# Weights of the values prepared one unit earlier through the projections' buffers, and the first loads of the values moved beside the first attention

## The chip, the core and the metric

The kernel is one program on one core of a Trainium2 chip. The metric is device time in microseconds (us). Before the change three runs gave 2971.14 us as the median, with 2968.95 and 2975.28 us at the ends. The profiled execution, from which all durations here come, took 2968.51 us.

## What is computed

The reference chains four blocks on an activation `x` of 8 sequences of 112 tokens with 512 channels, all in float32, and a context of 8 sequences of 375 tokens with 512 channels:

```
x = L0(x, ctx)        # cross attention, one head:  x + alpha * softmax(q k^T / sqrt(C)) v Wo
x = L1(x, ctx)        # layer norm, token mixing, a scan over time with a 16 x 16 state per head, channel mixing
x = L2(x, ctx)        # the same with other weights
x = L3(x, ctx, ctx)   # layer norm + cross attention (16 heads of 128, keys and values from ctx) twice, then an MLP
```

The change concerns L0, and the part of L3 that needs only the context: the values `ctx @ wv1`, `ctx @ wv2` (512 to 2048 columns each) and a group of the keys. They don't depend on `x`, so the kernel computes them as filler work while L1 and L2 run.

## The kernel before, in words

**The values (`values`, L818).** The generator covers five sets of weights: four pairs of groups of 512 columns of `wv1` and `wv2`, and one pair of `wk1`. A set has 12 units (the last has 3), one for each pair of sequences and third of their tokens, 51 in all. A unit multiplies 2 x 2 blocks with seven products in place of eight; the products are called k1, k6, k7, k2, k8, k5, k9. Each needs one operand of 256 x 512 from the weights (four raw blocks a11, a21, a22, a12, of which one is overwritten, and sums of them: a21 + a22, s1, s2, s3) and one block of the context. The context's blocks and their sums were written to memory during L0 by `park` (L249), and come back as `cv` tiles through `load` (L882). A product is two matmuls of 128x128 by 128x512 (L906). ACT copies its PSUM bank to SBUF (L931, L999, L1013), POOL adds copies (L932), and SP stores the results (L922 to L926). There are two PSUM banks, used in turn; k1, k6, k7 and k8 add up in one bank, with a copy out between them.

**The filler.** L1 and L2 call `fill(n)` at many points, and each call emits n pieces of the generator (one piece is one product with its copies). Inside `time_mix` (L549) a manual schedule makes all engines but SP follow the written order; elsewhere a planner decides each engine's order when the program is built. All engines execute their own queue in order. Every DMA is issued on SP's queue; they take eight semaphores in turn, so a transfer is issued only after the one eight before it has landed.

**A new set of weights.** Seven buffers `w` hold a set's operands. The first set is loaded by `weights(0)` (L841): four loads of 512 KB (L839), then four sums on POOL (L846 to L849). `weights(2)` does the same between L1 and L2. The other three changes of set happen in the middle of `time_mix` and are done by `relay` (L852): from the last-but-one unit of the old set on, three raw blocks lie in two buffers of the projections' pool `wpool` (four buffers of 128 x 2048), POOL writes a sum or a copy into a buffer of the old set as soon as that one's last product has been issued (L862, L864, L868, L874, and the copy L876), and three raw blocks are loaded a second time into freed buffers of `w`. `after` (L965) counts the products and triggers each step.

**The scan (`time_mix`).** There are 64 steps per layer: 4 groups of channels (`c`) with 16 steps (`at`). Per step, ACT copies `vp` to PSUM (L588, L589), DVE multiplies (L687) and scans (L691, `st`, two buffers), POOL multiplies `rs` (L695, six buffers), and every four steps PE sums four `rs` (L668, `ps_y`), always two steps behind. Each step also has one or two pieces of filler. From `at` = 2 of the next group on, the group norm of the finished one runs beside it (L607 to L634).

**L0 (`layer0`, L225).** Its pools, in order of their SBUF addresses: `keep` (identity, transposed weights, w_qk, q, z, w_vo), `work` (the context's tiles `cx`, four buffers, and small tiles), and in PSUM first the two `mm` banks, then the attention's six. After eight attentions the output projection `ps_o` (L161) runs in the two `mm` banks and DVE adds it to `x` (L350). When L0's pools close, the values' pool and its two banks take the lowest addresses.

## Time and profile before

| what | before |
|---|---|
| three runs: median (ends) | 2971.14 us (2968.95, 2975.28) |
| the profiled execution | 2968.51 us |
| its span | 2966.1 us (2.4 us lie around it) |
| PE (matmul) busy | 2861.6 us, 96% |
| DVE busy | 1610.9 us, 54% |
| ACT busy | 998.9 us, 34% |
| POOL busy | 876.4 us, 30% |
| mean DMA rate | 136 GB/s |
| granted TensorE clock, mean | 0.988 |
| L0's attentions and projection | 62 to 157 us |
| L1's 64 steps of the scan | 366 to 623 us |
| L2's 64 steps of the scan | 986 to 1247 us |

The profile gives, for each engine, when it was busy, how long it sat idle before an instruction and which engine or transfer ended that idle time. Matmul records are half-matmuls in this program: one matmul of 128x512 in float32 shows as two records, and a product of the values as four. A line of a timeline is: start, length, engine, source line, operation, output<-inputs, shape, count, and in brackets the idle time before it with its releaser.

### The profile page before, as it was taken

The page shows a single profiled execution, that of the slowest core. Times are in us where ns is not written, and L with a number is a line of the kernel's source. Part 1 is how long each engine was busy: PE and PEld are TensorE (multiplying, and loading weights), DVE is VectorE, ACT ScalarE, POOL GpSimd, SP SyncE. Part 2 cuts the span into 40 slices and gives each one's busy share as a digit, 9 for nine tenths or more (in the row PEclk, how much of TensorE's full clock was granted, in tenths as well). Part 3 has the DMA queues.
Part 4 walks back from the last instruction along what each step waited for, and adds up shares of the span by engine and source line. Part 5 has one row for each costly group of instructions (what it writes and reads, how often), then busy time and mean ns, then how long its engine had stood idle before and what let it go on. Part 6 is the DMA issues. An engine that isn't in the chain of part 4 may idle for free.

```text
span 2966.1 us, 29798 instructions
## 1 busy us (share of the span) xinstructions
PE 2861.6 (96%) x10130; PEld 1561.7 (53%) x10130; DVE 1610.9 (54%) x2350; ACT 998.9 (34%) x1992; POOL 876.4 (30%) x702
## 2 busy tenths in 40 slices
PE   8979999999999999999899999999999999999999
PEld 4734443344444433356465666666565656656544
DVE  1563288857342688743455554545554554545455
ACT  2123355533233555532332323232331323323311
POOL 2142078754231588732411010100302010000030
PEclk9989999999999999999999999999999999999999
DMA  6421398944321889742344344334233433432110
GB/s 255 150 89 45 116 291 247 282 135 126 96 68 54 246 251 271 225 141 70 130 130 128 129 128 129 108 119 140 88 120 102 144 108 119 140 114 77 42 54 25
DMA packets 199318, 402.90 MB, mean 136 GB/s; under 512 B 33288, under 2 KB 119592, under 8 KB 192384
## 3 DMA queue, kind: packets, MB, share of 16 engines
q1 hardware_dynamic: 199168, 401.01, 43.0%
q8 instruction: 81, 1.33, 0.2%
q14 instruction: 69, 0.57, 0.1%
HBM read 323.16 MB, written 77.91 MB: 135 GB/s over the span
## 4 chain that ended last, share of the span: by engine, by line
PE 80%; DVE 7%; POOL 4%; issue 3%; ACT 3%; DMA 2%; SPq 0%; DVEq 0%; POOLq 0%; ACTq 0%
PE ps_vk L906 13%; PE ps_k1k L1134 10%; PE ps_k5k L1134 7%; PE av L1303 6%; PE sc L1290 5%; PE ps_o L161 3%; PE pt L1293 3%; PE ps_fk L161 2%; PE ps_k1q L1061 2%; PE ps_k L484 2%; PE ps_r L484 2%; PE ps_k5q L1061 2%; PE ps_k7q L1061 2%; PE ps_fr L161 2%; PE ps_k5o L1061 1%
## 5 line engine op out<-in xcount | busy, mean ns | idle before, releaser
L906 PE MATMUL ps_vk<-wv,cv 128*128 128x512 f32 x1328 | 597.0, 600 | 29.5 <-DMA wv<-in_L_xattn_wv 8.2
L906 PEld LDWEIGHTS ps_vk<-wv,cv 128*128 128x128 f32 x1328 | 249.3, 191 | 361.7 <-issue 301.8
L932 POOL TENSOR_TENSOR k<-k,k 128x512 f32<-128x512 f32 (+1 forms) x153 | 201.7, 1318 | 306.7 <-ACT k L931 261.6
L691 DVE TENSOR_TENSOR_SCAN st<-decay,kv 128x904 f32<-128x904 f32 x128 | 260.7, 2037 | 16.7 <-POOL rs L695 4.0
L695 POOL TENSOR_TENSOR rs<-st,r 128x896 f32<-128x896 f32 x128 | 246.7, 1928 | 55.3 <-DVE st L691 42.4
L218 ACT ACTIVATE prob<-sc,top 112x376 f32<-112x376 f32 (+1 forms) x264 | 151.8, 575 | 322.6 <-DVE top L215 195.2
L1303 PEld LDWEIGHTS av<-pts,v 125*128 125x128 f32 (+1 forms) x1536 | 185.7, 193 | 31.0 <-DVE pts L1299 16.0
L1290 PE MATMUL sc<-k,q 128*112 128x376 f32 x512 | 201.1, 485 | 0.7 <-ACT prob L218 0.7
L1283 POOL COPY k<-over_k 128x4 f32<-128x4 f32 x64 | 13.8, 224 | 604.7 <-PE sc L1290 576.7
L1303 PE MATMUL av<-pts,v 125*128 125x112 f32 (+1 forms) x1536 | 190.0, 278 | 1.8 <-DVE pts L1299 0.9
L1134 PE MATMUL ps_k1k<-cs,wsk 128*128 128x375 f32 x480 | 178.6, 481 | 1.5 <-ACT p1k L1137 1.5
L215 DVE TENSOR_REDUCE top<-sc 112x1 f32<-112x376 f32 (+1 forms) x264 | 143.5, 545 | 64.3 <-PE sc L1290 51.9
L687 DVE TENSOR_TENSOR kv<-vp,k 128x904 f32<-128x904 f32 x128 | 141.5, 1105 | 64.8 <-ACT vp L589 59.0
L931 ACT COPY k<-ps_vk 128x512 f32<-128x512 f32 (+1 forms) x153 | 89.2, 583 | 183.1 <-PE ps_vk L906 180.2
L999 ACT COPY k<-ps_vk 128x512 f32<-128x512 f32 (+1 forms) x153 | 89.1, 582 | 153.6 <-PE ps_vk L906 148.7
L1293 PEld LDWEIGHTS pt<-ident_l,prob 112*125 112x125 f32 (+1 forms) x768 | 97.8, 176 | 72.0 <-DVE prob L220 43.9
L1293 PE MATMUL pt<-ident_l,prob 112*125 112x112 f32 (+1 forms) x768 | 121.4, 277 | 2.5 <-DVE prob L220 1.9
L220 DVE TENSOR_SCALAR prob<-prob,total 112x376 f32<-112x376 f32 (+1 forms) x264 | 118.3, 448 | 8.0
L1134 PEld LDWEIGHTS ps_k1k<-cs,wsk 128*128 128x128 f32 x480 | 89.5, 190 | 59.4 <-ACT p1k L1137 1.8
L589 ACT COPY vp<-vj 128x896 f32<-128x896 f32 x124 | 112.8, 910 | 7.0 <-DMA vj<-rows 3.1
L1141 DVE TENSOR_TENSOR k<-ps_k5k,u2k 128x375 f32<-128x375 f32 x52 | 28.5, 548 | 159.2 <-PE ps_k5k L1134 158.2
L1310 DVE TENSOR_TENSOR ctxt<-av,bv 128x448 f32<-128x448 f32 x64 | 39.9, 624 | 128.8 <-PE av L1303 128.8
(384 smaller groups left out, 4800.6 us busy)
## 6 DMA issues: line engine op xcount, KB each, us to landing
vj<-rows SPq DMA_DIRECT2D x124, 448.0 KB
cv<-blocks SPq DMA_DIRECT2D x181, 251.5 KB
cs<-blocks SPq DMA_DIRECT2D x120, 375.0 KB
wvs<-k SPq DMA_DIRECT2D x128, 256.0 KB
v<-wvs SPq DMA_DIRECT2D x64, 512.0 KB
cx<-in_ctxT SPq DMA_DIRECT2D x38, 750.0 KB
v<-wvs SPq DMA_DIRECT2D x64, 252.0 KB
wvs<-k SPq DMA_DIRECT2D x64, 224.0 KB
```

Of the source, the lines that this page charges most:

```text
L161: nc.tensor.matmul(p, w[:, k, o * P : (o + 1) * P], rhs(k, h), start=k == 0, stop=k == NC - 1)
L215: nc.vector.tensor_reduce(top, scores, AX.X, ALU.max, negate=True)
L218: nc.scalar.activation(prob, scores, AF.Exp, bias=top, accum_out=total)
L691: nc.vector.tensor_tensor_scan(flat(st), flat(decay[:, c]), flat(kv), 0.0, ALU.mult, ALU.add)
L695: nc.gpsimd.tensor_mul(by_batch(rs), st[:, :, :L], by_batch(r[:, c, :]))
L906: nc.tensor.matmul(to, left, right, start=start and n == 0, stop=k == 1, skip_group_check=True)
L932: nc.gpsimd.tensor_add(y, z, y)
L1061: nc.tensor.matmul(to, lhsT, rhs, start=start and k == 0, stop=k == 1, skip_group_check=not start)
L1134: nc.tensor.matmul(y, lhsT, rhs, start=start and k == 0, stop=k == 1, skip_group_check=True)
L1290: nc.tensor.matmul(sc, q[:, o, tok], kt[:, o, :], start=True, stop=True)
L1293: nc.tensor.transpose(pt[t][:nt, o, :], prob[:, t0 : t0 + nt], ident[:L, :L])
L1303: nc.tensor.matmul(av[:, o, :], v[:nt, t, o * HD : (o + 1) * HD], pts[:nt, t, o, :], start=t == 0, stop=t == 2,)
```

## The change

It does two things, and swaps two allocations.

1. In L0, the context's tiles get a pool of their own (`near`), which now has the lowest SBUF addresses; `z` and `w_vo` get a pool (`last`) behind `keep`; and in PSUM the attention's banks come before the `mm` banks. So the buffers and banks that the values' pool takes over are ones that the attention uses, not ones that the output projection uses.
2. For the changes of set that happen inside L1's and L2's scans with `at` = 0 and 2, `relay` is replaced by the new `ahead`, which starts one unit sooner (unit 9 of 12). It takes three buffers of `wpool`, loads the four raw blocks once, makes three sums there and one in the old k1's buffer, and then ACT copies six operands of 128 x 1024 from `wpool` into the old set's buffers, one after each of the following products. The next set's first products (k1, k6, k7, k2 of its first unit) read the operands in `wpool`. The change of set at `at` = 3 still uses `relay`.
3. In `time_mix`, `early` is allocated ahead of `w_o`.

```diff
         with (
+            tc.tile_pool(name="a0s", bufs=2, space=PSUM) as ps2,
+            tc.tile_pool(name="a0c", bufs=4) as near,
             tc.tile_pool(name="a0", bufs=1) as keep,
+            tc.tile_pool(name="a0z", bufs=1) as last,
             tc.tile_pool(name="a0w", bufs=2) as work,
             tc.tile_pool(name="a0p", bufs=2, space=PSUM) as ps,
-            tc.tile_pool(name="a0s", bufs=2, space=PSUM) as ps2,
...
-                cxs[b] = work.tile([P, NC, S], F32, tag="cx", name=f"cx0_{b}", bufs=4)
+                cxs[b] = near.tile([P, NC, S], F32, tag="cx", name=f"cx0_{b}")
...
-            z = keep.tile([P, NC, N], F32, name="z0")
+            z = last.tile([P, NC, N], F32, name="z0")
...
-            w_vo = product(turned(w_v, "v"), w_o, "w_vo")
+            w_vo = product(turned(w_v, "v"), w_o, "w_vo", last)
...
+        def ahead(at, old, new):
+            x1, x2, x3 = (wpool.tile([P, NC, C], F32, tag="w", name=f"wx{j}_{at}") for j in range(3))
+            a11, a21, a22, a12, s2, s1 = (x[:, k : k + 2] for x in (x1, x2, x3) for k in (0, 2))
+            for y, o, k in ((a11, 0, 0), (a21, 1, 0), (a22, 1, 1), (a12, 0, 1)):
+                raw(y, at, o, k)
+            new.update(k1=a11, k6=s1, k7=s2, k2=a12, k8=a22, k5=a21, k9=old["k1"])
+            yield "k7", 2
+            nc.gpsimd.tensor_sub(s2, a11, a21)
+            yield "k6", 0
+            nc.gpsimd.tensor_add(a21, a21, a22)
+            yield "k8", 0
+            nc.gpsimd.tensor_sub(s1, a21, a11)
+            yield "k1", 2
+            nc.gpsimd.tensor_sub(old["k1"], a12, s1)
+            free = [("k6", "k1"), ("k7", "k6"), ("k2", "k7"), ("k8", "k2"), ("k5", "k8"), ("k9", "k5")]
+            for last, _ in free:
+                yield last, 1
+                nc.scalar.copy(old[last], new[dict(free)[last]])
+            yield "k1", 0
+            new.update({what: old[last] for last, what in free})
...
-            if unit == UNITS - 2 and at != 1:
+            if unit == UNITS - 3 and at in (0, 2):
+                new = {}
+                steps = ahead(at + 1, s, new)
+                following = next(steps)
+                made.clear()
+            elif unit == UNITS - 2 and at == 3:
                 new = {}
                 steps = relay(at + 1, s, new)
                 ready = next(steps)
-            elif unit == UNITS - 1 and at != 1:
+            elif unit == UNITS - 1 and at == 3:
                 following = ready
                 made.clear()
```

More of the change, by code (lines that the diff above doesn't have):

```diff
@@ L291, in turned, with product @@
                 return t
-            def product(a, b, name, scale=1.0):
-                y = keep.tile([P, NC, C], F32, tag=name, name=name)
+            def product(a, b, name, pool, scale=1.0):
+                y = pool.tile([P, NC, C], F32, tag=name, name=name)
                 for c in range(NC):
@@ L303, in product @@
                 return y
-            w_qk = product(turned(w_q, "q"), turned(w_k, "k"), "w_qk", 1.0 / math.sqrt(C))
+            w_qk = product(turned(w_q, "q"), turned(w_k, "k"), "w_qk", keep, 1.0 / math.sqrt(C))
             q = keep.tile([P, NC, N], F32, name="q0")
-            z = keep.tile([P, NC, N], F32, name="z0")
+            z = last.tile([P, NC, N], F32, name="z0")
             project(
@@ L642, in beside @@
                 return {2: take(c - 1), 3: group_norm(c - 1, g)}
+            early = wpool.tile([P, NC, C], F32, tag="w", name=f"early{n}").rearrange("p k c -> p (k c)")
             w_o = wpool.tile([P, NC, C], F32, tag="w", name=f"w_{pre}Wo")
@@ L648, in time_mix @@
                 )
-            early = wpool.tile([P, NC, C], F32, tag="w", name=f"early{n}").rearrange("p k c -> p (k c)")
             for at in range(3):
```

## The prediction

> **What bounds the kernel now.** I read the page first, then who waited for whom on PE, and then the order of time around each long wait.

> ```profile
> PE 2861.6 (96%) x10130; PEld 1561.7 (53%) x10130; DVE 1610.9 (54%) x2350; ACT 998.9 (34%) x1992; POOL 876.4 (30%) x702
> PE 80%; DVE 7%; POOL 4%; issue 3%; ACT 3%; DMA 2%; SPq 0%; DVEq 0%; POOLq 0%; ACTq 0%
> ```

> PE is the bound nearly everywhere; some 104 us of the span are left to win. The change adds no matmul, so it can only shorten PE's pauses or add to them. In PE's table of waits these belong to the code it touches:

> ```profile
> PE ps_vk L906 <- DMA wv<-in_L_xattn_wv: 8.2, 1, 8.2
> PE ps_vk L906 <- POOL wv L868: 4.8, 2, 2.7
> PE ps_vk L906 <- POOL wv L848: 2.3, 1, 2.3
> PE ps_vk L906 <- POOL wv L876: 1.6, 1, 1.6
> ```

> PE's timeline behind L0's output projection:

> ```profile
> 157.31 0.92 PE L182 MATMUL mean_ln<-part_mean_ln,mean_c 128*128 128x448 f32 x2
> 166.38 2.05 PE L906 MATMUL ps_vk<-wv,cv 128*128 128x512 f32 x2 [8.15 <-DMA wv<-in_L_xattn_wv]
> 168.22 1.70 PE L182 MATMUL var_ln<-part_var_ln,mean_c 128*128 128x448 f32 x2
> 169.71 3.49 PE L906 MATMUL ps_vk<-wv,cv 128*128 128x512 f32 x6
> 175.52 7.30 PE L906 MATMUL ps_vk<-wv,cv 128*128 128x512 f32 x16 [2.32 <-POOL wv L848]
> 186.35 5.91 PE L447 MATMUL ps_t<-xx,maa 128*128 128x448 f32 x8 [3.53 <-DVE xx L438]
> ```

> The filler's first product stands in PE's queue ahead of `var_ln`, so its late weights hold up L1's layer norm too: 14 us of idle in all, at a granted clock of 0.79 (windows, 159 to 186.35).

> **Part 1, the first loads.** SP issued the four `cv` and four `wv` loads from 157.54 on, when `ps_o` had ended, and the first sum began at 167.66: 10.1 us later. In the order of the changed program the first `cv` load waits for the last transposition of the attention (about 130.5), with SP's queue empty since 110. So the operands land near 141, the four sums run until about 151, and at 157.3 PE has work. The constants behind them on SP (4 rows for the biases, 6 for the heads) come earlier; the 14 loads of `maa` and `d`, now behind all these, end near 158 (0.6 us each from 149) and are needed at 177.

> Then the chain, by the rows of before. `mean_ln` now waits for the last addition to `x` (157.51 + 0.68): 158.3 to 159.2. DVE's subtraction 2.0, ACT's squares 1.7, DVE's sum 1.9: 165.1. PE meanwhile runs four products (0.43 us a record, a copy of 0.58 between those that share a bank), so `var_ln` comes at about 165.5. Table load and root 1.9 on ACT, behind two copies: 168.2. Reciprocal 2.94, multiplication 2.0: 173.5. ACT's scaling stands behind the copy of k6 of the second unit and starts at 174.1; before, it started at 183.01. That is 8.9 us, and everything to the mixing follows it (POOL `sx`, DVE `xx`, `ps_t` at 177.5). PE has seven matmuls fewer left beside the mixing, but DVE sets the pace there (22 us of work in 195 to 218), so that costs nothing; if DVE were faster, it would cost 7 x 0.86 = 6.0.

> What it costs: the sums now lie beside `ps_o`. DVE before:

> ```profile
> 170.61 5.34 DVE L180 TENSOR_TENSOR part_mean_ln<-part_mean_ln,x 128x448 f32<-128x448 f32 x2
> 182.91 0.27 DVE L809 TENSOR_TENSOR less_mean_h<-ident_rs,mean_h 128x128 f32<-128x128 f32 x1
> ```

> Two additions that take 0.62 each elsewhere (L178) took 2.67 each while POOL made the same sums. [...] In the new order two additions of the layer norm and two `over` lie between additions to `x` from 143 to 151, and `less_mean_h`, which waits for four small loads, behind them. PE has two banks and 3 us a group, so 2.3 us of lateness is free. If one addition is blocked the projection loses nothing; if each of three is, `x` of the fourth group comes at 151.8 in place of 146.2 and PE loses about 3.4. I take 2.0. The DMA wait's whole 14 us can't be had, since DVE and ACT are late next. Part 1: 8.9 - 2.0 and about 0.6 for DVE pauses in the mixing: **-7.5** (bounds -5 and -10.5).

> **Part 2, the changes of set.** What they cost now is best read from the starts of `ps_y`, one batch for each four steps:

> ```profile
> 1037.10 1.71 PE L668 MATMUL ps_y<-rs,pick 128*32 128x448 f32 x16
> 1052.67 1.71 PE L668 MATMUL ps_y<-rs,pick 128*32 128x448 f32 x16
> ...
> 1101.53 1.71 PE L668 MATMUL ps_y<-rs,pick 128*32 128x448 f32 x16
> 1104.65 1.98 PE L906 MATMUL ps_vk<-wv,cv 128*128 128x512 f32 x4 [1.41 <-ACT k L1013]
> 1108.80 10.55 PE L906 MATMUL ps_vk<-wv,cv 128*128 128x512 f32 x20 [2.16 <-POOL wv L868]
> 1119.18 1.88 PE L906 MATMUL ps_vk<-wx,cv 128*128 128x512 f32 x4
> 1122.67 1.98 PE L906 MATMUL ps_vk<-wv,cv 128*128 128x512 f32 x4 [1.61 <-POOL wv L876]
> 1124.58 1.71 PE L668 MATMUL ps_y<-rs,pick 128*32 128x448 f32 x16
> ```

> In L2 the batch with the change takes 23.05, the same place in another group 15.57: 7.5 us lost. In L1 (497.55 to 519.97, against 433.17 to 452.65) it is 22.42 against 19.48: 2.9 lost. So 10.4 us is the most that can be had.

> Per change POOL loses the copy (1.04) and keeps four sums of 2.35; they move about 20 us earlier, one for each two steps, between the `rs`. There POOL is 77% busy (93 of 120 us in 370 to 490), so two steps of 7.7 leave 1.8: each sum is 0.6 too much, and idle between `rs` is not all usable.

> L1: following POOL's new order from 470.6, `rs` of step 15 ends at 499.9 instead of 494.9. DVE's scan waits for it (two `st` buffers), and PE's batch of 497.55, which has two steps of slack, waits 2.3. It then runs at 503.1 what started at 503.85: a gain of 0.7, and ACT's blocked group norm takes some. I take **-0.5** (bounds +2 and -2.9).

> L2: the same reckoning puts the multiplication that releases ACT (3.88 us idle at 1103.37) 1.5 later, so the wait of 1.41 at 1104.65 becomes 2.9; but the waits for L868, the hidden 1.7 in the row of 10.55, and L876 go. Six ACT copies come in. The trace has the same form at L416, 128x1024 in 1.05 us. A step has two evictions (1.16) and `vp` (1.1): 3.3 with one copy, 4.4 with two, against PE's 3.9. Behind a copy stand the next eviction and `vp`, for which PE and DVE wait; at the one step with two copies and the norm, PE resumes at 1109.0, no sooner than before, and only the later 3.3 us are won. I take **-3.0** (bounds 0 and -7.5). All twelve copies on PE's path would be +12.6; none, 0.

> The raw loads come earlier into buffers that have been free since 380, and three loads of 512 KB per change fall away; SP's later `fWk` and `Wfk` loads have over 100 us. In `weights(2)` a11 is now the block whose buffer comes free last: the four sums end perhaps 8 us later than 727.7, under the channel mixing, which runs on PE until 786. Swapping `early` and `w_o` costs nothing either: PE has filler at the start of the scan. If those covers were gone it would be those 8 us.

> Sum: -7.5 - 0.5 - 3.0 = **-11**. The profiled execution (2968.5) lies 2.6 under the median; I set it on the median: 2971.1 - 11 = **2960.1**.

> **Rivals.** *Everything goes* (0.15): no blocking in L0 (-10) and POOL's and ACT's gaps hold all moved work (-10.4): 2951. For it: POOL's mean share is 30%. Against it: it was saturated from 490 to 518.
> *Only the loads pay* (0.17): `less_mean_h` and the blocked additions cost the full 3.4, so -5.5, and the scan gives back 2: 2967.6. For it: ACT's and POOL's queues each held PE up by 1.4 to 2.7 us at these places. Against it: the longest waits go whole.
> *Slower* (0.05): POOL becomes the scan's bound. Its idle of 0.2 to 1.4 us ahead of each `rs` waits for DVE and can't be filled, so all eight sums (18.8) lie on the loop of scan and `rs`, with half of each copy (6.3) behind them: 25.1 - 10.4 - 7.5 = +7, 2978. It decides from about seven and a half sums on the loop.
> That the loads don't move is excluded by the order of the program.

> **Numbers.** The forecast holds 0.63, its own range 2953 to 2965. Within 0.2% (5.9 us, about what a measurement can tell here) means 2965.2 to 2977.1: mostly the second rival. Faster 0.78, same 0.17, slower 0.05. The range 2951.5 to 2969 leaves out the tail of the first rival and the slower cases.

> **What would show it.** Right: no wait of `ps_vk` for `wv` near 160; the first sum near 141; `ps_t` near 178 to 180; `ps_o` ending 1 to 3 us late with stretched additions on DVE; no L868 or L876 waits before 1300; the L2 batch at 18 to 21 us, the L1 batch near 22 with a wait of `ps_y` for `rs`. Wrong: ACT copies far off 1.05; `vp` waits of DVE at every step with a copy; `ps_t` after 183.

## The result, and the profile after

Eight runs of the changed kernel have a median of 2957.48 us (2954.9 to 2966.74), eight of the kernel before, on the same chip, 2969.68 us (2966.97 to 2975.28). The ratio is 0.9966 with a 95% interval of 0.9955 to 0.9976: 10.1 us faster (7 to 13); the two medians lie 12.2 us apart, inside this interval. The forecast was 11 us. The profiled execution took 2960.41 us, its span 2958.3 us, 7.8 us shorter than before. Why a single pair of profiles shows less than the runs is said under "Right and wrong".

The page's busy times and the engines' shares of the chain that ended last:

```profile
PE 2862.2 (97%) x10130; PEld 1561.7 (53%) x10130; DVE 1603.7 (54%) x2350; ACT 1009.1 (34%) x2004; POOL 872.6 (29%) x700
PE 80%; DVE 7%; POOL 4%; DMA 3%; issue 3%; ACT 3%; SPq 0%; DVEq 0%; POOLq 0%; ACTq 0%
```

PE's work is the same; ACT has twelve instructions and 10 us more (the copies). In PE's table of waits the four lines shown of before are gone. ACT's three lines (`ps_vk` for `k`) have grown from 12.5 us to 14.1 in sum. Of the lines that are new or grew, these two belong to the changed code as well:

```profile
PE ps_o L161 <- DVE x L353: 3.6, 1, 3.6
...
PE ps_y L671 <- POOL rs L698: 3.3, 3, 1.6
```

PE's timeline behind L0's output projection (lines are three higher than before):

```profile
133.47 14.46 PE L161 MATMUL ps_o<-z,w_vo 128*128 128x448 f32 x38
151.56 10.98 PE L161 MATMUL ps_o<-z,w_vo 128*128 128x448 f32 x24 [3.63 <-DVE x L353]
...
163.32 1.02 PE L182 MATMUL mean_ln<-part_mean_ln,mean_c 128*128 128x448 f32 x2
...
182.32 1.02 PE L450 MATMUL ps_t<-xx,maa 128*128 128x448 f32 x2 [1.28 <-DVE xx L441]
```

The waits of 8.15 and 2.32 us, shown in the prediction, have gone, and `ps_t` comes 19.0 us behind `mean_ln`, where it came 29.0 us behind it. But `mean_ln` itself comes 6 us later. The projection waits for DVE, and DVE's timeline shows why:

```profile
142.68 2.73 DVE L180 TENSOR_TENSOR part_mean_ln<-part_mean_ln,x 128x448 f32<-128x448 f32 x1
145.33 5.58 DVE L979 TENSOR_TENSOR over<-over,bv 4x512 f32<-4x512 f32 x2
150.84 0.67 DVE L353 SCALAR_TENSOR_TENSOR x<-ps_o,alpha,x 128x448 f32<-128x448 f32 x1
```

POOL's timeline of the same stretch, with the second and the last of its four sums (139.92 to 150.37):

```profile
142.58 2.35 POOL L850 TENSOR_TENSOR wv<-wv,wv 128x1024 f32<-128x1024 f32 x1
...
147.70 2.67 POOL L852 TENSOR_TENSOR wv<-wv,wv 128x1024 f32<-128x1024 f32 x1
```

Three DVE instructions with two SBUF inputs (one addition, two subtractions `over`) end only about half a microsecond after one of POOL's sums ends. The `x` behind them, for which PE needs the bank, comes 5.9 us late; 2.3 of that are free, as the forecast said, and PE waits 3.6. In L2 the batch with the change of set:

```profile
1091.65 2.12 PE L671 MATMUL ps_y<-rs,pick 128*32 128x448 f32 x16
1095.67 1.98 PE L933 MATMUL ps_vk<-wv,cv 128*128 128x512 f32 x4 [1.91 <-ACT k L1045]
...
1110.36 1.71 PE L671 MATMUL ps_y<-rs,pick 128*32 128x448 f32 x16
```

It takes 18.71 us in place of 23.05; the waits for POOL are gone, those for ACT have stayed.

### The profile page after: what moved, and what is told of

Its sections match the earlier page's. It is cut to its first block, busy times and chain, and to the rows that moved or that the text cites. A ratio compares the mean times of both kernels' runs of the same rounds, so it can differ in the third digit from the quotient of the medians.

```text
span 2958.3 us, 29826 instructions
## 1 busy us (share of the span) xinstructions
PE 2862.2 (97%) x10130; PEld 1561.7 (53%) x10130; DVE 1603.7 (54%) x2350; ACT 1009.1 (34%) x2004; POOL 872.6 (29%) x700
## 4 chain that ended last, share of the span: by engine, by line
PE 80%; DVE 7%; POOL 4%; DMA 3%; issue 3%; ACT 3%; SPq 0%; DVEq 0%; POOLq 0%; ACTq 0%
PE ps_vk L933 13%; PE ps_k1k L1166 10%; PE ps_k5k L1166 7%; PE av L1335 6%; PE sc L1322 5%; PE pt L1325 3%; PE ps_o L161 3%; PE ps_fk L161 2%; PE ps_k1q L1093 2%; PE ps_r L487 2%; PE ps_k L487 2%; PE ps_k7q L1093 2%; PE ps_fr L161 2%; PE ps_k5q L1093 2%; PE ps_k5o L1093 1%
## 5 line engine op out<-in xcount | busy, mean ns | idle before, releaser
L933 PE MATMUL ps_vk<-wv,cv 128*128 128x512 f32 x1296 | 583.7, 601 | 13.9 <-ACT k L1031 6.3
L218 ACT ACTIVATE prob<-sc,top 112x376 f32<-112x376 f32 (+1 forms) x264 | 151.8, 575 | 322.3 <-DVE top L215 194.8
L1031 ACT COPY k<-ps_vk 128x512 f32<-128x512 f32 (+1 forms) x153 | 89.1, 582 | 163.2 <-PE ps_vk L933 156.0
L1173 DVE TENSOR_TENSOR k<-ps_k5k,u2k 128x375 f32<-128x375 f32 x52 | 28.5, 548 | 159.2 <-PE ps_k5k L1166 158.2
```

What stands on the lines that cost most here:

```text
L218: nc.scalar.activation(prob, scores, AF.Exp, bias=top, accum_out=total)
L933: nc.tensor.matmul(to, left, right, start=start and n == 0, stop=k == 1, skip_group_check=True)
```

## The experiments

Eleven kernels were run, each beside runs of the kernel before on its own chip. Microseconds from a ratio are (1 - ratio) x 2970; the intervals are 3 to 5 us wide to either side. So the causes are read from stages of the traces, between landmarks that all kernels have: the first record of `ps_o` (it lies among the last attention's products, 3.6 us ahead of the long row of `ps_o`), the first `mean_ln`, the first `ps_t`, L1's first `ps_y`; and in each scan the stretch from the fourth to the thirteenth `ps_y`, which holds the change of set.

| kernel | ratio to before (95%) | `ps_o` to `mean_ln` | to `ps_t` | to `ps_y` | L1 stretch | L2 stretch |
|---|---|---|---|---|---|---|
| before | 1 | 26.91 | 29.04 | 202.26 | 151.53 | 156.18 |
| changed | 0.9966 (0.9955, 0.9976) | 33.44 | 19.00 | 199.22 | 152.32 | 152.99 |
| p1_loads_only | 0.9975 (0.9961, 0.9988) | 31.01 | 19.01 | 197.56 | 151.56 | 155.84 |
| p2_sets_only | 0.9985 (0.9973, 0.9997) | 26.91 | 29.16 | 202.39 | 151.41 | 152.79 |
| l2_only | 0.9956 (0.9940, 0.9971) | 34.63 | 19.00 | 201.27 | 153.19 | 152.05 |
| l1_only | 0.9981 (0.9967, 0.9995) | 31.75 | 19.00 | 197.52 | 151.25 | 155.83 |
| over_pool | 0.9957 (0.9942, 0.9973) | 35.30 | 19.06 | 200.83 | 152.57 | 152.45 |
| over_first | 0.9953 (0.9936, 0.9970) | 31.95 | 19.01 | 197.71 | 151.25 | 154.98 |
| sums_dve | 0.9945 (0.9928, 0.9962) | 27.96 | 18.99 | 201.14 | 151.51 | 154.94 |
| dve_l2 | 0.9953 (0.9936, 0.9971) | 28.84 | 18.99 | 199.59 | 151.20 | 152.63 |
| dve_loads | 0.9957 (0.9941, 0.9974) | 27.96 | 18.98 | 201.01 | 152.76 | 155.85 |
| copies_dma | 1.0023 (1.0013, 1.0033) | 29.84 | 19.00 | 199.15 | 160.78 | 162.43 |
| copies_twice | 0.9978 (0.9968, 0.9989) | 33.44 | 19.00 | 201.31 | 153.45 | 154.58 |

### Each part alone: p1_loads_only, p2_sets_only

```diff
 # p1_loads_only: the new pools of layer0, and
+            if unit == UNITS - 2 and at != 1:
+                new = {}
+                steps = relay(at + 1, s, new)
 # p2_sets_only: layer0 as before, ahead() for at in (0, 2), early ahead of w_o
```

> The first loads moved beside the first attention, all three changes of set inside the scans as in the kernel before. Theory (each part keeps its own gain): the first ps_y of L1 comes 7.1 us sooner than in the kernel before, as in the changed kernel; the L1 change keeps its batch of 22.4 us and the L2 change its batch of 23.1 us, so the whole is 7 us faster (5 to 9). Rival (the loads' gain is lost again where a later wait takes its place, and the changed kernel's gain comes from the changes of set): 0 to 3 us faster.

Measured: 7.4 us faster (4 to 12). The scans are those of the kernel before, as in the theory. L1's first `ps_y` comes 10.6 us sooner, counted from `ps_o`, 3.5 more than the theory had; 2.9 of these come between the second `var_ln` and the second `ps_t`, where this trace has no slower clock (see "Right and wrong").

> The new changes of set in L1 and L2 and the swap of early and w_o; L0 as in the kernel before, with its wait of 8.1 us for wv. Theory: L1's change gives nothing or loses 0.8 us, L2's gives 3.2 us, so 2 to 3 us faster, and the first ps_y of L1 within 0.5 us of the kernel before. Rival (the loss in L1 in the changed kernel comes from the shifted phase of the loads, not from the new change of set): L1's change gains 0.5 to 3 us here and the whole is 4 to 6 us faster.

Measured: 4.5 us faster (1 to 8). L1's stretch is 151.41 against 151.53, L2's 152.79 against 156.18, as the theory had them; the rival's gain in L1 did not come. The two parts alone add up to 11.9 us, the whole gave 10.1: they add up within what is measured.

### The change of set in one layer alone: l2_only, l1_only

```diff
-            if unit == UNITS - 3 and at in (0, 2):
+            if unit == UNITS - 3 and at in (2,):   # l1_only: (0,)
...
-            elif unit == UNITS - 2 and at == 3:
+            elif unit == UNITS - 2 and at in (0, 3):   # l1_only: (2, 3)
```

> The changed kernel with the old change of set in L1 and the new one in L2 alone. Theory (the new change costs 0.8 us in L1): 0.5 to 1 us faster than the changed kernel, about 11 us faster than the kernel before. Rival (the batches around L1's change are longer because of the earlier start, not because of the copies): slower than the changed kernel by 0.5 to 2.9 us, the batch of L1's change back at 22.4 us.

Measured: 13.1 us faster than before (9 to 18), 3 us more than the changed kernel, with overlapping intervals. The theory had 11. L1's stretch, with the old change of set, was the longest so far, 153.19, which seems to speak against the theory. But PE's clock was halved behind its wait for POOL there (PE's window: from, to, length, busy time, records, granted clock, DMA share, GB/s):

```profile
499.60:503.00 3.40, 3.28 (x4) 0.50 0.86 250
```

That costs 1.7 us, and the batch took 24.08 where the kernel before took 22.42. The trace decides nothing about L1.

> The changed kernel with the new change of set in L1 alone; L2 has the old one. Theory: the stretch of L1 takes 151 to 152.6 us and that of L2 156.0, so it is as fast as the loads alone within 1 us: 7 us faster than before, 2.6 slower than the changed kernel. Rival (L1's change costs 3 us): 3 to 5 us faster than before.

Measured: 5.6 us faster (1.5 to 10). The stretches came as the theory had them (151.25 and 155.83); the time lies between the two. So over all traces: L1's stretch is 152.05 as the mean of the five with the old change (151.20 to 153.19), 151.72 of the six with the new one and single ACT copies (151.25 to 152.57): -0.3, smaller than its own scatter. The scatter of the old change is the clock: 151.20 to 151.56 in the three traces without half clock in this stretch, 152.76 and 153.19 in the two (dve_loads, l2_only) that have 3.4 us of it. So where the clock stays up, the new change gains nothing in L1; it only takes away the wait of 2.7 us for POOL, behind which the clock fell in two of five traces. L2's is 155.93 in four (155.83 to 156.18) and 153.26 in seven (152.05 to 154.98): -2.7, outside its scatter.

### What held up the projection: over_pool, over_first, sums_dve

```diff
 # over_pool
-            nc.vector.tensor_sub(over, over, bv)
+            nc.gpsimd.tensor_sub(over, over, bv)
 # over_first: loads and subtraction of over stand ahead of load(m) and weights(0), the stores stay behind
 # sums_dve
-            nc.gpsimd.tensor_sub(s2, a11, a21)
...
+            eng = nc.gpsimd if at else nc.vector
+            eng.tensor_sub(s2, a11, a21)
...
```

> The changed kernel with the two small subtractions of the values' biases (over, 4x512) on POOL behind its four sums, where DVE made them between the additions to x of L0's projection. Theory (DVE's two-input instructions stand blocked behind POOL's sums and hold up the last addition to x, for which PE waited 3.6 us): that wait goes, ps_o ends near 157 in place of 162.4, ps_t of the mixing starts 3 to 5 us sooner, and the whole is 3 to 5 us faster than the changed kernel. Rival (POOL's reads slow down DVE's additions to x themselves, or the clock of PE sets the end): ps_o ends after 160.5 and the time is within 1.5 us of the changed kernel.

Measured: `mean_ln` came 35.30 us behind the first `ps_o`, later than in the changed kernel (33.44) and in all six traces with its L0 (29.84 to 34.63); the time is 12.8 us under before, not to be told from the changed kernel's. The stall had not gone, it had moved. SP's timeline and ACT's:

```profile
153.04 0.26 SPq L981 DMA_DIRECT2D overs<-over  x1
...
157.61 0.31 ACT L811 ACTIVATE mean_h<-same 128x128 f32<-128x128 f32 x1 [22.53 <-DMA same<-in_heads]
```

The stores of `over` now wait on SP for POOL (until 153.0), and three of the four loads `same` of the heads stand behind them in SP's queue; ACT's `mean_h` waits for these, DVE's `less_mean_h` for ACT, and the next `x` behind it in DVE's queue for that. The run says nothing for or against the theory; it shows the chain of queues.

> The changed kernel with the loads and the two subtractions of the biases (over) ahead of the loads of the first set; the stores of over stay behind. So they run before POOL's sums, and the loads of the heads no longer stand behind a store that waits for over. POOL's sums come about 2 us later, near 142 to 152. Theory (three blocked instructions in a row held up the additions to x): only additions of the layer norm and the copies of pick stand beside the sums, at most one between two additions to x; PE's wait for DVE x is under 1.5 us and ps_t 3 to 5 us sooner than in the changed kernel. Rival (any instruction that reads SBUF is stretched, pick too, and two of them lie between two additions to x): the wait stays at 2 to 4 us and nothing is gained.

Measured: 14.0 us faster than before (9 to 19). PE's wait is 2.14 us and `mean_ln` comes at 31.95, only 1.5 us sooner than in the changed kernel and inside the range of the six traces with its L0. With `over` out of the way, other instructions of DVE stretched in its place, and not only ones with two inputs:

```profile
147.96 2.37 DVE L807 COPY ones_t<-heads 128x128 f32<-128x128 f32 x1
150.25 2.62 DVE L816 COPY pick<-heads 128x32 f32<-128x32 f32 x4
```

In the changed kernel, behind POOL's last sum, they take 0.20 and 0.46. The rival is right in this: these copies from SBUF to SBUF were stretched too.

> The changed kernel with the four sums of the first set of weights made by DVE in place of POOL. A DVE sum of 128x1024 is taken at 1.16 us (the multiplication of 128x1792 takes 2.02), and between two additions to x of the projection DVE has 2.3 us free. Theory (what the changed kernel lost on ps_o is POOL's reads blocking DVE's two-input instructions, and the slower clock after PE's pause): no wait of ps_o for DVE above 1 us, ps_o 27 to 28 us from its first record to mean_ln (33.4 in the changed kernel, 26.9 before), no addition above 0.8 us, ps_t 5 to 6 us sooner and the whole 5 us (3 to 6) faster than the changed kernel. Rival (the sums wait for the late operands at about 141 and hold DVE's queue, whichever engine makes them): ps_o still 30 us or more, and the time within 2 us of the changed kernel.

Measured: 16.3 us faster than before (11 to 21). PE's timeline, and DVE's:

```profile
134.25 23.59 PE L161 MATMUL ps_o<-z,w_vo 128*128 128x448 f32 x62
```

```profile
141.95 1.22 DVE L851 TENSOR_TENSOR wv<-wv,wv 128x1024 f32<-128x1024 f32 x1
143.08 0.62 DVE L178 TENSOR_TENSOR part_mean_ln<-x 128x448 f32<-128x448 f32 x1
```

The projection runs through without a wait, a DVE sum takes 1.22 us (POOL 2.35 to 2.67), no addition is stretched (the one of `part_mean_ln` takes 0.62, each `over` 0.67), and `mean_ln` comes 27.96 us behind the first `ps_o`: 1.05 more than before, which is the filler's product that stands ahead of it. The theory holds: the stall was POOL's sums against DVE.

### What the copies on ACT cost: copies_dma, copies_twice

```diff
-                nc.scalar.copy(old[last], new[dict(free)[last]])
+                nc.sync.dma_start(old[last], new[dict(free)[last]])      # copies_dma
+                nc.scalar.copy(old[last], new[dict(free)[last]])         # copies_twice: this line twice
```

> The changed kernel with the six copies per change of set made by DMA from SBUF to SBUF in place of ACT, in L1 and L2. If ACT's copies are what is left of the cost of the new change of set (1.05 us each, in ACT's queue ahead of evictions and vp), the four batches of ps_y around L1's change take 1 to 3 us less (152.3 us from the fourth ps_y to the thirteenth in the changed kernel) and so do those of L2 (153.0), and the whole is 2 to 5 us faster. Rival (SP's queue and the DMA engines, 90% busy in the scans, pay for it): vj and cv come late, the scan waits for DMA, and it is 1 to 6 us slower.

Measured: 6.8 us slower than before (4 to 10), some 17 slower than the changed kernel. PE's waits in L1's scan, then in L2's:

```profile
PE ps_vk L933 <- DMA wv<-wx: 4.1, 1, 4.1
```

```profile
PE ps_vk L933 <- DMA wv<-wx: 7.6, 1, 7.6
```

Both stretches grew by 9 us, the waits and the half clock behind them (6.8 us of it in L1's stretch, 10.2 in L2's). The rival was right in kind and too small: the copies by DMA come late for the product that needs them. This run can't show what ACT's copies cost, since they were replaced by something dearer.

> The changed kernel with each of the six ACT copies per change of set issued twice, 12.6 us more of ACT in all. If the copies lie on the path (all of each), it is 12 us slower; if they lie half in ACT's gaps, 4 to 8 us; if ACT has room enough, within 2 us. The forecast's reckoning (3.3 us of ACT for a step with one copy, 4.4 with two, against PE's 3.9) says: about half a microsecond for each doubled copy, 6 us slower, equally in L1 and L2.

Measured: 6.5 us faster than before (3 to 10), 3.6 slower than the changed kernel. The stretches grew by 1.7 us in L1 (153.45 against a mean of 151.72) and 1.3 in L2 (154.58 against 153.26), 3.0 for twelve more copies of 1.05 us: 0.25 us each. It is one trace, and L2's mean has a scatter of 3 us; against the two L2 traces that, like this one, have no half clock there (152.99, 152.05), it is 2.1, which makes 0.3 each. So a quarter to a third of an added copy reaches PE, where the forecast's reckoning had half; the rest lies in ACT's gaps. What the first copy costs need not be the same.

### Combinations: dve_l2, dve_loads

```diff
 # dve_l2 = sums_dve with ahead for at == 2 alone; dve_loads = sums_dve with relay in all three places
```

> The changed kernel with the first set's sums on DVE, and the new change of set in L2 alone (L1 has the old one). Theory (in L1 the new change gains and loses nothing: from the fourth to the thirteenth ps_y 151.8 us with it and 152.1 without, as means over the traces so far): within 1.5 us of the kernel with DVE sums and both changes, 15 to 17 us faster than the kernel before. Rival (in L1 it costs 3 us, as the measured times of the changed kernel and of the one with L2 alone would have it): 18 to 20 us faster than the kernel before.

Measured: 14.0 us faster (9 to 19), a little less than the theory's 15 to 17; L1's stretch 151.20, L2's 152.63. No sign of 3 us that L1's change would cost.

> The moved first loads with the sums on DVE, and all changes of set as before: part 1 with its cost on the projection taken away. Theory: mean_ln comes 28.0 us after the first record of ps_o, ps_t 19.0 later, and what follows as in the kernel before or up to 4 us shorter; the scans as before (152.1 and 156.0). So 9 us from mean_ln to ps_t less the product ahead of it, and 1 to 4 in the mixing: 10 to 13 us faster than before. Rival (the sums on DVE only move the loss to the layer norm): 5 to 8 us faster.

Measured: 12.8 us faster (8 to 18). Part 1 without its cost is about 10.5 us by the stages (258.3 from `ps_o` to `ps_y` before, 247.4 to 248.1 in the three kernels with DVE sums). The theory holds.

The version with DVE sums and both changes of set has the lowest ratio of all, 0.9945. Its interval overlaps with that of the changed kernel, so that it beats it is shown by the stage (5.5 us less from `ps_o` to `mean_ln` than in the changed kernel's trace, 4.4 less than the mean of the traces with POOL sums), not by the times alone.

## Right and wrong, step by step

**Part 1, forecast -7.5, measured -7.6.** This is the stage from `ps_o` to L1's first `ps_y`: 258.3 before (two traces), 250.7 as the mean of the six traces with the changed kernel's L0 (247.6 to 254.9). The sum was right, two of its terms were not: one was 2.4 us too good, one 2.4 too bad. That they cancelled is luck.

- *The chain from `mean_ln` to `ps_t`*: forecast 19.2 us (158.3 to 177.5), measured 18.98 to 19.06 in all eleven traces that have the moved loads. Right, and the steadiest number of the study. The order of waits was right too: behind the DMA stand DVE and ACT.
- *The stall of the projection*: forecast 2.0, bound 3.4. Measured, over the 27.96 of the kernel without the conflict: 4.4 us as the mean of six (1.9 to 6.7). This is the term that was mis-sized. The 2.0 was the author's choice, and no run shows it as a fixed cost; what the runs showed in its place is the 4.4. That DVE's instructions stretch beside POOL's sums was right to the row: an addition of 0.62 took 2.73, two `over` of 0.67 took 5.58. All three were stretched, the case for which the forecast wrote 3.4, and the wait was 3.63. It went wrong twice. It took a value between one stretched and three, where five of the six traces have at least three stretched; PE's wait is 3.2 us in the mean (1.5 to 3.7). And it counted PE's pause only, not what comes after it: the 24 records behind the wait took 10.98 us, where 24 of `ps_o` take about 9.1 at full clock; that is another 1.1 in the mean, and it comes and goes from trace to trace. So `ps_o` ended some 5 us late, where 1 to 3 had been forecast, and `ps_t` came at 182.3 instead of 178 to 180.
- *The mixing*: forecast -0.6, since the sum of -7.5 comes out only with the 0.6 as a gain; measured -1.0 to -4.8 (mean -3.0). The forecast also said that fewer products beside the mixing would be worth nothing, since DVE sets the pace. But each product brings POOL an addition, and POOL's additions held DVE up. DVE's and POOL's lines of before:

```profile
214.10 3.06 DVE L462 TENSOR_TENSOR xg<-xg,xa 128x448 f32<-128x448 f32 x2
```

```profile
215.04 1.65 POOL L932 TENSOR_TENSOR k<-k,k 128x512 f32<-128x512 f32 x1
```

and of after:

```profile
210.97 1.15 DVE L465 TENSOR_TENSOR xg<-xg,xa 128x448 f32<-128x448 f32 x2
```

```profile
208.11 1.27 POOL L959 TENSOR_TENSOR k<-k,k 128x512 f32<-128x512 f32 x1 [0.21 <-ACT k L958]
```

Before, POOL made its additions beside DVE's last `xg`, and two of these took 3.06; now POOL is done by 209.4 and they take 1.15. That is 1.9 of the 2.2 us between `ps_mg` and the second `var_ln`. The remaining scatter of this stage, up to 3 us, lies between that `var_ln` and the second `ps_t`, and it is the clock. This part takes 20.05 us in the three traces without half clock in it (p1_loads_only, l1_only, over_first), 21.5 to 21.7 in three with 3.1 to 3.4 us of it, and 22.9 to 23.1 in seven with 6.0 to 6.5, both traces with the old L0 among them. Of the mean of -3.0 some 1.4 lie here; two traces of the old L0 can't tell whether the change brought that or chance.

**Part 2, L1, forecast -0.5, measured -0.3** (scatter larger, so no gain is shown). The form was right: the batch is 21.83 in place of 22.42, and a `ps_y` waits for `rs`, 0.73 us where 2.3 was forecast. Against that stand waits for ACT of 1.31 in this batch, where 0.6 is usual, and 1.74 in the next.

**Part 2, L2, forecast -3.0, measured -2.7.** The batch came to 18.71 (forecast 18 to 21; 18.71 to 19.84 in the seven traces). As forecast, ACT's wait of 1.4 became longer (1.91), and the POOL waits of 2.16 and 1.61 went. An added copy cost 0.25 to 0.3 us where the reckoning had some 0.5; but part of the batch's gain of 4.3 was lost again later: in the changed kernel the second batch after the change takes 15.99 us, where 13.86 is usual, and 19.0 in the two traces (over_first, sums_dve) in which the clock fell there.

**The edits costed at nothing** stayed at nothing: no wait of PE at the change of set between the layers, none for `early` and `w_o`.

**The rivals.** *Only the loads pay* was wrong at L2 and right at L1. *Everything goes*, with its 10 us for an L0 without blocking, is what the kernels with DVE sums reach in part 1 (10.5 us); in the scans 3.0 of its 10.4 us went. *POOL as the scan's bound* did not show: waits of `ps_y` for `rs` are 2.3 us in L1's scan, 1.0 in L2's.

**Why the profiled pair differs by 7.8 only.** In the changed kernel's trace the lead is 13.1 us when L2's scan ends. From the thirteenth `ps_y` of L2 to the second `var_ln` of L3 it then takes 252.2 us, the kernel before 246.7. In all traces this stretch lies between 246.7 and 252.7, without order by kernel (246.7 is the least). Of the 5.5 us, 2.1 are a transfer of `cy`, for which PE waited 2.5 us in one execution and 0.4 in the other, 1.8 a wait of `mean_ln` for DVE (2.50 and 0.72), and 1.7 half clock (10.2 us of it against 6.8 behind the wait of 4.12 in L3). So 5.5 us of the difference between these two profiles is scatter, which the medians average out.

## What to carry to other kernels

Before work is moved beside other work, list what each engine does in that window, and ask of DVE's instructions whether POOL's run beside them: here an addition of 0.62 us took 2.73 beside POOL's sums of 2.35 to 2.67, and the same sums on DVE itself took 1.22 and made PE wait for 0.27 at the longest (dve_l2). A pause of PE is to be priced with the slower clock that may come behind it: here 1.7 us more in the changed kernel, 2.9 in l2_only, nothing in p1_loads_only. Where one profile of each kernel is compared, compare stages between common landmarks, since whole spans scatter by more than a change of 0.3%.

## What the runs showed of the hardware

**A pause can cost twice, and the granted clock shows when.** PE's window behind the wait of 3.63 us in the changed kernel's projection (from, to, length, busy time, records, granted clock, DMA share, GB/s):

```profile
151.60:162.40 10.80, 10.80 (x25) 0.84 0.58 139
```

```profile
149.59:153.00 3.41, 1.44 (x4) 1.00 0.10 17
153.00:156.41 3.41, 3.41 (x6) 0.50 0.72 194
```

```profile
147.07:150.49 3.42, 1.64 (x5) 1.00 0.01 2
150.49:153.90 3.41, 1.57 (x4) 1.00 0.08 18
```

```profile
148.09:151.50 3.41, 0.81 (x3) 1.00 0.03 7
151.50:154.91 3.41, 2.32 (x3) 0.50 0.10 22
154.91:158.33 3.42, 3.42 (x6) 0.50 0.87 228
```

| kernel | wait for DVE | most idle time in one stretch | half clock behind it |
|---|---|---|---|
| copies_dma | 1.52 | 1.4 | none |
| p1_loads_only | 2.90 | 1.8 | none |
| l1_only | 3.63 | 1.8 | none |
| changed | 3.63 | 2.0 | 3.4 |
| over_first | 2.14 | 2.1 | 3.4 |
| copies_twice | 3.63 | 2.2 | 3.4 |
| over_pool | 3.14 | 2.5 | 6.8 |
| l2_only | 3.69 | 2.6 | 6.8 |

The records show the half clock too: in the changed kernel's projection 6 lie in a filled stretch of it, 10 or 11 in one at full clock. So half clock came, at this place, where a stretch held about 2 us of idle time or more, and not up to 1.8; it lasted a second stretch where the first still began with idle time (1.1 us in l2_only, 0.7 in over_pool). That holds for this place alone: the clock also fell behind the narrow matmuls of the mixing (32x448), with PE busy for 3.30 of 3.40 us (194.0 to 197.4 in the changed kernel), and stood at half until 207.6.

**Copies with one input were stretched too.** In over_first `ones_t`, a DVE copy of 128x128 from SBUF to SBUF, took 2.37 us beside POOL's sums and 0.20 in the changed kernel. The forecast had counted on additions and subtractions alone. The additions to `x`, with one input from PSUM, kept their 0.67 to 0.69 in the traces of the changed kernel, over_first, sums_dve and copies_dma; in over_first one of 0.68 (at 145.41) ran beside a sum of POOL's of 2.61.
